# A two-layer graph attention network on one core: one-hot matrices made six at a time, and more edge tiles in two exact parts

## The chip, the core and the metric

The kernel runs on one core of a Trainium2 chip. The core has TensorE (PE, with its weight loads shown apart as PEld), VectorE (DVE), ScalarE (ACT), GpSimd (POOL) and SyncE (SP), which run their own instruction queues in order and wait for one another through semaphores; 16 DMA engines move data between the device memory and the core's SBUF. The metric is device time in microseconds of one execution; lower is better.

## The reference, cut to what matters

The graph has N = 3125 nodes and E = 53125 edges, which are sorted by their target node `dst`. Node features have 768 columns.

```python
h = relu(layernorm(x))
h1 = relu(layer_norm(gat(h, W1, heads=4, 256 columns each))) + h @ Wr1 + br1
out = x + layer_norm(gat(h1, W2, heads=1, 768 columns)) + h1 @ Wr2 + br2

def gat(x, W, ...):
    xl = x @ W
    e = leaky_relu(alpha_src[src] + alpha_dst[dst], 0.2)
    alpha = softmax of e over the edges of one dst        # per head
    return segment_sum(xl[src] * alpha, dst) + bias       # the aggregation
```

The change is in the last line, the aggregation: for every edge the row `xl[src]` is fetched, weighted with the edge's `alpha`, and added to the row of its target node.

## The kernel before, in words

The nodes are cut into NB = 25 blocks of P = 125. Since the edges are sorted, the edges of a block lie in one stretch, and a window of S = 2304 edges, J = 18 tiles of 128, covers it. Edges in the window that belong to other blocks drop out, as their target number relative to the block matches no column.

The function `sums` does the aggregation for both layers, with a loop over the 25 blocks and in it one over the 18 tiles. For one tile `c = b * J + j`:

- L525: POOL issues an indirect DMA that gathers the 128 rows `xl[src]` of the tile from `table` (layer 1: 1024 columns, 4 KB a row; layer 2: 768 columns, 3 KB a row) into a buffer `g`. The row numbers are a column of `idx_s`, which lies in SBUF. Layer 1 has 10 such buffers, layer 2 has 18. Once a block (j = 2) a small indirect DMA `ao` (L531) goes the same way, and once a block SP loads the block's own rows (`own`).
- L536: DVE makes the one-hot matrix `oh` (128 edges x 128 columns) by comparing `iota_f` with the tile's column of `rel_s`, the targets relative to the block. Layer 1 has 8 buffers, layer 2 has 14.
- A tile in two exact parts (`split(j)` true): ACT writes `hi` = `g` x alpha, rounded to the type float32r (L543, four instructions in layer 1, one per head, and one in layer 2); DVE writes the remainder `g` x alpha - `hi` back into `g`, also as float32r (L544, as many instructions). PE multiplies `oh` with the two halves of `hi` and the two halves of `g` (L548), four matmuls, and adds all into the block's PSUM tile `pa`.
- Any other tile: a weight matrix `w` = one-hot x alpha is made, in layer 1 by ACT from `oh`, one per head (L558), in layer 2 by DVE from `iota_f`, `rel_s` and alpha in one instruction (L555), and PE multiplies `w` with `g` in plain float32 (L560). A float32 matmul stands in the trace as two records.

Before the change, layer 1 has one such other tile in each block (j = 8), layer 2 five of 18 (j = 0, 4, 8, 12, 16).

After a block's tiles PE adds the bias (L564). Then `finish` runs for the block while the next block's tiles go on: DVE adds the self-loop (`z`, L512), and layer normalisation follows (L317 to L327). In layer 1, `end1` normalises (L797), transposes on PE (L806), applies relu on ACT (L808), adds the residual on DVE (`h1T`, L810) and multiplies by `W2` on PE (L819); beside it PE works off the residual product `h @ Wr1` for the later blocks (L774), which ends some five blocks before the layer does. In layer 2, `end2` does two instructions of DVE over 768 columns (L908, L909) and stores the result; beside it PE works off the residual product `h1 @ Wr2` of 16 blocks (L853), which DVE adds in L862.

The order on the engines is a scheduler's in layer 1, which places instructions by its own estimates. In layer 2 PE, ACT and DVE keep the order of the program (`lag` is 5: `finish` begins five tiles into the next block), so an instruction that waits holds up all that is queued behind it.

Of the kernel before, what the change touches and what calls it, by code (L numbers as in the profile page):

```python
# [9 lines left out]
F32 = mybir.dt.float32  # L10
F32R = mybir.dt.float32r
# [3 lines left out]
AF = mybir.ActivationFunctionType  # L15
OP = mybir.AluOpType
# [42 lines left out]
def in_order(  # L59
# [16 lines left out]
    nc = tc.nc  # L76
    N, D = x.shape
    E = src.shape[0]
    H, C1 = a_src1.shape
    HC = H * C1  # L80
    C2 = W2.shape[1]
    P = 125
# [10 lines left out]
    table1 = dram.tile([N, HC], F32, name="table1")  # L93
    table2 = dram.tile([N, C2], F32, name="table2")
# [3 lines left out]
    alo1_d = dram.tile([128 * NB * J, H + 1], F32, name="alo1_d")  # L98
    alo2_d = dram.tile([128 * NB * J, 2], F32, name="alo2_d")
# [17 lines left out]
    iota_f = const.tile([128, 128], F32, name="iota_f")  # L117
# [6 lines left out]
    rel_s = const.tile([128, NB * J], F32, name="rel_s")  # L124
# [11 lines left out]
    def load_rows(q, t, src_, b):  # L136


        if b < NB - 1:
            q.dma_start(t, src_[b * P:b * P + 128, :])  # L140
        else:
            q.dma_start(t[:112], src_[b * P:b * P + 112, :])
            q.dma_start(t[112:P], src_[b * P + 112:(b + 1) * P, :])
# [27 lines left out]
    def bias_rows(pool, o, n, name):  # L171
        t = pool.tile([2, n], F32R, name=name)
        nc.sync.dma_start(t.bitcast(F32), parts_d[:, o:o + n])
        return t
# [311 lines left out]
    def sums(heads, cols, table, al, alo_d, bias, split, ahead, his, lag, gp, pp, end, more=iter(())):  # L486

        width = heads * cols  # L490
        f = width // 2
        n = min(cols, f)
        assert split(0) or n == f
        running = []

        def step():
            for g in list(running):
                if next(g, running) is running:
                    running.remove(g)
            next(more, None)  # L500

        def finish(b, own, pa, ao):
            for _ in range(lag):
                yield

            iso = gp.tile([P, 1], F32, name="iso", bufs=2)
            nc.vector.tensor_tensor(iso, ao[:P, heads:], node_f[:P, b:b + 1], OP.not_equal)
            aw = gp.tile([P, heads], F32, name="aw", bufs=2)
            nc.vector.tensor_scalar(aw, ao[:P, :heads], iso, None, op0=OP.max)
            z = gp.tile([P, width], F32, name="z", bufs=2)  # L510
            for o in range(0, width, n):
                nc.vector.scalar_tensor_tensor(z[:, o:o + n], own[:P, o:o + n], aw[:, o // cols:o // cols + 1],  # L512
                                               pa[:, o // f, o % f:o % f + n], op0=OP.mult, op1=OP.add)
            yield from end(b, z)

        with tc.manual_schedule(engines={PE, ACT, DVE}) if lag else nullcontext():
            for b in range(NB):
                own = gp.tile([128, width], F32, name="own", bufs=3 if lag else 2)
                pa = pp.tile([P, 2, 512], F32, name="pa", bufs=2)
                ao = gp.tile([128, heads + 1], F32, name="ao", bufs=3)  # L520
                for j in range(J):
                    c = b * J + j
                    g = gp.tile([128, width], F32R, name="g", bufs=ahead)
                    gf = g.bitcast(F32)
                    nc.gpsimd.indirect_dma_start(  # L525
                        out=gf, out_offset=None, in_=table[:, :],
                        in_offset=bass.IndirectOffsetOnAxis(ap=idx_s[:, c:c + 1], axis=0))
                    if j == 6:
                        load_rows(nc.sync, own, table, b)
                    if j == 2:  # L530
                        nc.gpsimd.indirect_dma_start(  # L531
                            out=ao, out_offset=None, in_=alo_d[:, :],
                            in_offset=bass.IndirectOffsetOnAxis(ap=at_last[:, b:b + 1], axis=0))
                    if split(j) or heads > 1:
                        oh = gp.tile([128, 128], F32R, name="oh", bufs=max(his, 4) + 4)
                        nc.vector.tensor_scalar(oh, iota_f, rel_s[:, c:c + 1], None, op0=OP.is_equal)  # L536
                    if split(j):

                        hi = gp.tile([128, width], F32R, name="hi", bufs=his)
                        for h in range(heads):  # L540
                            cs = slice(h * cols, (h + 1) * cols)
                            a = al[:, j, h, b:b + 1]
                            nc.scalar.activation(hi[:, cs], gf[:, cs], AF.Copy, scale=a)  # L543
                            nc.vector.scalar_tensor_tensor(g[:, cs], gf[:, cs], a, hi[:, cs].bitcast(F32),  # L544
                                                           op0=OP.mult, op1=OP.subtract)
                        for t in (hi, g):
                            for i in range(2):
                                nc.tensor.matmul(pa[:, i, :f], oh[:, :P], t[:, i * f:(i + 1) * f],  # L548
                                                 start=(j == 0 and t is hi), stop=False)
                    else:  # L550
                        w = gp.tile([128, heads, P], F32, name="w", bufs=6 if lag else 4)
                        for h in range(heads):
                            a = al[:, j, h, b:b + 1]
                            if heads == 1:
                                nc.vector.tensor_scalar(w[:, h, :], iota_f[:, :P], rel_s[:, c:c + 1], a,  # L555
                                                        op0=OP.is_equal, op1=OP.mult)
                            else:
                                nc.scalar.activation(w[:, h, :], oh[:, :P].bitcast(F32), AF.Copy, scale=a)  # L558
                        for o in range(0, width, n):
                            nc.tensor.matmul(pa[:, o // f, o % f:o % f + n], w[:, o // cols, :], gf[:, o:o + n],  # L560
                                             start=(j == 0), stop=False)
                    if j == J - 1:
                        for i in range(2):
                            nc.tensor.matmul(pa[:, i, :f], ones_r, bias[:, i * f:(i + 1) * f],  # L564
                                             start=False, stop=True)
                    step()
                running.append(finish(b, own, pa, ao))
            while running:
                step()


    with tc.tile_pool(name="m1", bufs=1) as mp:
        al1 = mp.tile([128, J, H, NB], F32, name="al1")
# [9 lines left out]
        with tc.tile_pool(name="w1", bufs=1) as wp, tc.tile_pool(name="pm1", bufs=1, space=PSUM) as pm1:  # L583
# [131 lines left out]
            with tc.tile_pool(name="pq1", bufs=1, space=PSUM) as pp:  # L715
# [11 lines left out]
                with tc.tile_pool(name="wf", bufs=2) as fp:  # L727
# [3 lines left out]
                    for k in range(NK2):  # L731
                        w2k = fp.tile([128, C2], F32, name="w2k")
                        nc.sync.dma_start(w2k, W2[k * 128:(k + 1) * 128, :])
                        for i in range(2):
                            t = fp.tile([128, C2], F32, name="w2t")
# [14 lines left out]
        with tc.tile_pool(name="w2", bufs=1, reuse_waits="tile") as wp, tc.tile_pool(name="e1", bufs=2, reuse_waits="tile") as ep, \  # L750
                tc.tile_pool(name="g1", bufs=1, reuse_waits="tile") as gp, tc.tile_pool(name="pg1", bufs=1, space=PSUM) as pp:
            w2 = wp.tile([128, NK2, R2], F32, name="w2")
            b1_r = bias_rows(wp, 0, HC, "b1_r")
# [30 lines left out]
            def later():  # L784
                for gi in range(1, NG):
                    yield from residual(gi)
# [5 lines left out]
            def end1(b, z):  # L792
# [32 lines left out]
                        nc.vector.tensor_copy(asad2[:, b, :], pm[:, 384:n])  # L825
                store_rows(nc.sync, table2, b, row)

            sums(H, C1, table1, al1, alo1_d, b1_r, lambda j: j % 18 != 8, 10, 4, 0, gp, pp, end1, later())


    with tc.tile_pool(name="m2", bufs=1, reuse_waits="tile") as mp, \
            tc.tile_pool(name="pr2", bufs=1, space=PSUM, reuse_waits="tile") as pr:
        al2 = mp.tile([128, J, 1, NB], F32, name="al2")
# [63 lines left out]
        more = rest()  # L897

        with tc.tile_pool(name="w3", bufs=1, reuse_waits="tile") as wp, tc.tile_pool(name="e2", bufs=2, reuse_waits="tile") as ep, \
                tc.tile_pool(name="g2", bufs=1, reuse_waits="tile") as gp, tc.tile_pool(name="pg2", bufs=1, space=PSUM, reuse_waits="tile") as pp:  # L900
            b2_r = bias_rows(wp, HC, C2, "b2_r")
            g2_b = wp.tile([P, C2], F32, name="g2_b")
            nc.sync.dma_start(g2_b, bcast(g2, C2))

            def end2(b, z):
                yield from norm_steps(ep, z, C2, 4)
                mu, rstd = norm_steps.found
                nc.vector.scalar_tensor_tensor(z, z, mu, g2_b, op0=OP.subtract, op1=OP.mult)  # L908
                nc.vector.scalar_tensor_tensor(z, z, rstd, xrs[b][:P], op0=OP.mult, op1=OP.add)  # L909
                for _ in range(3):  # L910
                    yield
                store_rows(nc.scalar, out, b, z)

            with tc.issue_after(behind):
                sums(1, C2, table2, al2, alo2_d, b2_r, lambda j: j % 18 not in (0, 4, 8, 12, 16), 18, 10, 5, gp, pp, end2, more)


@with_exitstack
# [469 lines left out]
```

## Time and profile before

| | |
|---|---|
| median of 10 runs | 2423.2 us (2418.51 to 2432.86) |
| the profiled execution | 2423.38 us, span 2421.6 us, mean granted clock 0.955 |
| PE busy | 2233.5 us (92%) |
| DVE busy | 1973.5 us (81%) |
| ACT busy | 1291.9 us (53%) |
| POOL busy | 1188.6 us (49%) |
| DMA | 637.97 MB, mean 263 GB/s |

The stages by time from the span's start: the dense products and softmax of layer 1 up to 512 us, the aggregation of layer 1 from 512 to 1512 us, the softmax of layer 2 up to 1712 us, the aggregation of layer 2 up to the end.

The profile is of one execution. A line of a group names source line, engine, operation, output <- inputs, shapes and count, then the busy time in us and the mean duration of one in ns, then the idle time of the engine just before them with what ended most of it. "issue" is a wait that ended with nothing that the profile shows. Matmuls overlap with their successors, so the duration of one is longer than the time to the next one's start; where the pace of PE matters, the time from start to start is what counts.

### The profile page before, as it was taken

Reading aid. Unit: us, or ns where it says so; the run is one execution under the profiler, and the core shown is the slowest. Engines: PE = TensorE matmul, PEld = TensorE weight load, DVE = VectorE, ACT = ScalarE, POOL = GpSimd, SP = SyncE. Lnnn points to the kernel's source line nnn. Section 1 sums busy time; section 2 is a strip of 40 time slices with the busy share of each in tenths; the row PEclk is TensorE's granted clock in tenths of the full one; section 3 lists DMA queues with packets and bytes.
Section 4 is the critical chain, followed back from the end, with each engine's and each line's share of the span. In section 5 each row is a group of like instructions: output and inputs, shape, how many; then the busy total and the mean of one; then the engine's idle time right before and its main releaser. Section 6 shows DMA issues by size and latency. Waiting matters only on the chain. (4 is left out here: it accounts for less than half of the span.)

```text
span 2421.6 us, 35879 instructions
## 1 busy us (share of the span) xinstructions
PE 2233.5 (92%) x11154; PEld 1457.4 (60%) x11154; DVE 1973.5 (81%) x4429; ACT 1291.9 (53%) x2687; POOL 1188.6 (49%) x1043
## 2 busy tenths in 40 slices
PE   5898999969999999999999999799799999998997
PEld 2565665435666666666666756575466666665665
DVE  6835999678999999989898999587577787777777
ACT  1231333137888888888888987001344444444443
POOL 2100000126756766565555764000577777777774
PEclk8998999989999999999999999799899999998999
DMA  5452552488899898988988986884688898888886
GB/s 182 153 202 91 181 190 62 149 286 295 303 314 305 293 333 292 329 289 309 311 303 284 347 301 223 311 308 143 227 310 307 305 320 303 293 297 302 281 292 212
DMA packets 185691, 637.97 MB, mean 263 GB/s; under 512 B 32170, under 2 KB 49435, under 8 KB 184724
## 3 DMA queue, kind: packets, MB, share of 16 engines
q0 software_dynamic: 109072, 437.23, 53.4%
q1 hardware_dynamic: 72570, 188.75, 22.4%
q10 hardware_dynamic: 3850, 9.60, 1.1%
q8 instruction: 93, 1.52, 0.3%
q14 instruction: 106, 0.87, 0.1%
HBM read 567.40 MB, written 68.08 MB: 262 GB/s over the span
## 5 line engine op out<-in xcount | busy, mean ns | idle before, releaser
L525 POOL DMA_INDIRECT g<-table,idx_s x900 | 1081.0, 1201 | 545.4 <-PE pa L548 296.9
L543 ACT ACTIVATE hi<-g,al 128x256 fp32r<-128x256 f32 (+1 forms) x2025 | 1004.8, 574 | 462.3 <-DMA g<-table,idx_s 183.3
L544 DVE SCALAR_TENSOR_TENSOR g<-g,al,hi 128x256 fp32r<-128x256 f32 (+1 forms) x2025 | 1032.2, 561 | 75.4 <-issue 44.1
L548 PE MATMUL pa<-hi,oh 128*125 128x512 f32 (+1 forms) x1500 | 611.7, 487 | 27.9 <-issue 18.9
L548 PE MATMUL pa<-g,oh 128*125 128x512 f32 (+1 forms) x1500 | 471.1, 389 | 26.0 <-issue 13.1
L548 PEld LDWEIGHTS pa<-hi,oh 128*125 128x125 f32 x1500 | 280.9, 191 | 222.9 <-issue 96.4
L548 PEld LDWEIGHTS pa<-g,oh 128*125 128x125 f32 x1500 | 279.4, 190 | 94.9 <-DVE g L544 28.3
L853 PE MATMUL pr<-wr,h 128*125 128x384 f32 x800 | 303.7, 510 | 16.8 <-issue 13.1
L819 PE MATMUL p<-w,h1T 128*125 128x384 f32 (+1 forms) x800 | 298.0, 492 | 1.8 <-DVE h1T L810 1.5
L645 PE MATMUL pm<-w,h 128*125 128x512 f32 x600 | 284.7, 625 | 0.0
L774 PE MATMUL pr<-h0k,wr 128*128 128x500 f32 (+1 forms) x576 | 257.8, 536 | 17.2 <-DMA h0k<-h0T_d 17.0
L536 DVE TENSOR_SCALAR oh<-iota_f,rel_s 128x128 fp32r<-128x128 f32 x775 | 207.2, 280 | 72.6 <-PE pa L548 71.6
L560 PE MATMUL pa<-g,w 128*125 128x384 f32 (+1 forms) x700 | 243.0, 475 | 13.4 <-ACT w L558 6.9
L853 PEld LDWEIGHTS pr<-wr,h 128*125 128x125 f32 x800 | 152.1, 195 | 105.4 <-issue 36.4
L819 PEld LDWEIGHTS p<-w,h1T 128*125 128x125 f32 x800 | 147.9, 188 | 81.2 <-issue 9.8
L645 PEld LDWEIGHTS pm<-w,h 128*125 128x125 f32 x600 | 114.1, 198 | 126.9 <-issue 126.2
L146 POOL DMA_DIRECT2D table<-row x25 | 16.0, 639 | 349.2 <-ACT row L648 322.2
L560 PEld LDWEIGHTS pa<-g,w 128*125 128x125 f32 x700 | 131.1, 193 | 85.2 <-issue 21.3
L774 PEld LDWEIGHTS pr<-h0k,wr 128*128 128x128 f32 x576 | 105.0, 191 | 60.2 <-DMA h0k<-h0T_d 18.0
L512 DVE SCALAR_TENSOR_TENSOR z<-own,aw,pa 125x256 f32<-125x256 f32 (+1 forms) x150 | 69.9, 521 | 75.9 <-PE pa L548 26.8
L392 PEld LDWEIGHTS <-ohs 125*128 125x128 bf16 x2700 | 101.8, 98 | 47.9 <-DVE ohs L380 32.2
L392 PE MATMUL pq<-tabs,ohs 125*128 125x100 bf16 (+1 forms) x2700 | 105.4, 192 | 22.0 <-DVE ohs L380 19.8
(198 smaller groups left out, 1648.6 us busy)
## 6 DMA issues: line engine op xcount, KB each, us to landing
bd<-dst_d SPq DMA_DIRECT2D x50, 576.0 KB
bs<-slo_d SPq DMA_DIRECT2D x50, 576.0 KB
g<-table,idx_s POOLq DMA_INDIRECT x900
r1T_d<-rt SPq DMA_DIRECT2D x100, 125.0 KB
r1t<-r1T_d SPq DMA_DIRECT2D x25, 500.0 KB
h1T_d<-h1T SPq DMA_DIRECT2D x25, 500.0 KB
h<-h1T_d SPq DMA_DIRECT2D x25, 500.0 KB
own<-table SPq DMA_DIRECT2D x24, 512.0 KB
```

Of the source, the lines that this page charges most:

```text
L392: nc.tensor.matmul(q[:, j], ohs[:P, (j0 + j) * 128:(j0 + j + 1) * 128], tabs[:, i], start=(i == 0), stop=(i == 2))
L512: nc.vector.scalar_tensor_tensor(z[:, o:o + n], own[:P, o:o + n], aw[:, o // cols:o // cols + 1], pa[:, o // f, o % f:o % f + n], op0=OP.m ...
L525: nc.gpsimd.indirect_dma_start(out=gf, out_offset=None, in_=table[:, :], in_offset=bass.IndirectOffsetOnAxis(ap=idx_s[:, c:c + 1], axis=0))
L536: nc.vector.tensor_scalar(oh, iota_f, rel_s[:, c:c + 1], None, op0=OP.is_equal)
L543: nc.scalar.activation(hi[:, cs], gf[:, cs], AF.Copy, scale=a)
L544: nc.vector.scalar_tensor_tensor(g[:, cs], gf[:, cs], a, hi[:, cs].bitcast(F32), op0=OP.mult, op1=OP.subtract)
L548: nc.tensor.matmul(pa[:, i, :f], oh[:, :P], t[:, i * f:(i + 1) * f], start=(j == 0 and t is hi), stop=False)
L560: nc.tensor.matmul(pa[:, o // f, o % f:o % f + n], w[:, o // cols, :], gf[:, o:o + n], start=(j == 0), stop=False)
L645: nc.tensor.matmul(pm[:P], h0[gi][:, k, o:o + P], w1[:, k, i * 512:(i + 1) * 512], start=(k == 0), stop=(k == NK1 - 1))
L774: nc.tensor.matmul(pm[:, :nb * P], wr1[:, k, m * 128:(m + 1) * 128], loaded[gi, k][:, :nb * P], start=(k == 0), stop=(k == NK1 - 1))
L819: nc.tensor.matmul(pm[:, :n], hT[:, k, :], w2[:, k, o:o + n], start=(k == 0), stop=(k == NK2 - 1))
L853: nc.tensor.matmul(pm[:, :384], h1[:, k, :], wr2[:, k, i * 384:(i + 1) * 384], start=(k == 0), stop=False)
```

## The change

The one-hot matrices of six tiles are made by one comparison, a `tensor_tensor` over 6 x 125 columns, with `iota_f` repeated six times and six columns of `rel_s` each repeated 125 times. There are 3 buffers for six tiles each, in both layers, in place of 8 and 14 for one. Each one-hot matrix has 125 columns in place of 128. The comparison is made for every tile, also for those of layer 2 that do not use it. In layer 1 all 18 tiles are now in two parts; in layer 2 all but three (j = 2, 8, 14). `w` has 4 buffers in place of 6 in layer 2.

```diff
-                    if split(j) or heads > 1:
-                        oh = gp.tile([128, 128], F32R, name="oh", bufs=max(his, 4) + 4)
-                        nc.vector.tensor_scalar(oh, iota_f, rel_s[:, c:c + 1], None, op0=OP.is_equal)
+                    if j % 6 == 0:
+
+                        ohs = gp.tile([128, 6, P], F32R, name="oh", bufs=3)
+                        nc.vector.tensor_tensor(ohs, iota_f[:, None, :P].to_broadcast([128, 6, P]),
+                                                rel_s[:, c:c + 6, None].to_broadcast([128, 6, P]), OP.is_equal)
+                    oh = ohs[:, j % 6, :]
...
-                                nc.tensor.matmul(pa[:, i, :f], oh[:, :P], t[:, i * f:(i + 1) * f],
+                                nc.tensor.matmul(pa[:, i, :f], oh, t[:, i * f:(i + 1) * f],
...
-                        w = gp.tile([128, heads, P], F32, name="w", bufs=6 if lag else 4)
+                        w = gp.tile([128, heads, P], F32, name="w", bufs=4)
...
-                                nc.scalar.activation(w[:, h, :], oh[:, :P].bitcast(F32), AF.Copy, scale=a)
+                                nc.scalar.activation(w[:, h, :], oh.bitcast(F32), AF.Copy, scale=a)
...
-            sums(H, C1, table1, al1, alo1_d, b1_r, lambda j: j % 18 != 8, 10, 4, 0, gp, pp, end1, later())
+            sums(H, C1, table1, al1, alo1_d, b1_r, lambda j: True, 10, 4, 0, gp, pp, end1, later())
...
-                sums(1, C2, table2, al2, alo2_d, b2_r, lambda j: j % 18 not in (0, 4, 8, 12, 16), 18, 10, 5, gp, pp, end2, more)
+                sums(1, C2, table2, al2, alo2_d, b2_r, lambda j: j % 18 not in (2, 8, 14), 18, 10, 5, gp, pp, end2, more)
```

## The prediction

> **What bounds the kernel now.** I first cut the span into its stages with the table of windows: the start of layer 1's aggregation (512 to 568 us), its steady part (568 to 1331), its tail after the residual products have run out (1331 to 1512), the softmax of layer 2 (1512 to 1712), layer 2's aggregation (1712 to the end). Columns are the busy us of PE, PEld, DVE, ACT and POOL, then granted clock, DMA share and GB/s.
>
> ```profile
> 568.00:1331.00 763.00, 755.97 (x2697) 485.38 (x2696) 693.32 (x1914) 651.39 (x1619) 476.94 (x370) 1.00 0.90 308
> 1331.00:1512.00 181.00, 172.76 (x690) 117.82 (x690) 172.76 (x480) 160.75 (x410) 112.67 (x82) 0.98 0.84 293
> 1712.00:2422.00 710.00, 634.90 (x2395) 442.88 (x2394) 533.47 (x1057) 303.38 (x349) 514.51 (x471) 0.93 0.86 292
> ```
>
> In the steady part of layer 1, PE is busy 99% at full clock. That alone is weak, since matmuls overlap, so I read who waits for whom in that window:
>
> ```profile
> POOL g L525 <- PE pa L548: 209.0, 204, 2.2
> ACT hi L543 <- PE pa L548: 71.3, 69, 2.8
> DVE oh L536 <- PE pa L548: 51.6, 67, 2.2
> PE pa L560 <- ACT w L558: 4.8, 8, 1.3
> ```
>
> Three engines wait for PE; PE itself waits 4.8 us for the `w` of the one tile per block that goes the fp32 way. PE is the bound there. DVE, at 91%, is next.
>
> Layer 2 is another matter. The groups of that window show 447 gathers, and the waits of POOL there show how little it is held up:
>
> ```profile
> L525 POOL DMA_INDIRECT g<-table,idx_s x447 | 486.5, 1088 | 168.1 <-issue 95.7 <-PE pa L548 33.3 <-remote 15.8
> POOL g L525 <- issue: 95.7, 314, 0.3
> POOL g L525 <- PE pa L548: 33.3, 56, 2.6
> ```
>
> POOL issues one gather of 128 rows after another, about 1.09 us each with 0.305 us between: 471 x (1.092 + 0.305) = 658 of 710 us. It waits for PE 33 + 5 us. So gather issue sets layer 2's pace, with the PE and DVE loop just behind it. Last, the timeline shows what makes an issue long (start us, us):
>
> ```profile
> 1952.27 0.95 POOL L525 DMA_INDIRECT g<-table,idx_s  x1 [0.30 <-issue]
> 1957.29 1.02 DVE L909 SCALAR_TENSOR_TENSOR z<-z,bn_rs,xr 125x768 f32<-125x768 f32 x1
> 1957.39 1.74 POOL L525 DMA_INDIRECT g<-table,idx_s  x1 [0.30 <-DVE z L908]
> ```
>
> An undisturbed issue takes 0.95 us. The second one began while a DVE instruction on two SBUF tensors ran until 1958.31, and ended 0.82 us after that. From start and end times, 110 of the 456 issues between 1730 and 2400 us end 0.82 us after an L544 ends and are longer by 54 us together; 30 do so after an L536, by 2.2 us.
>
> **The change, part by part.**
>
> PE, layer 1: 25 tiles (j = 8) leave the fp32 path. In the chain, `PE pa L560 x8` takes 1.73 us up to the next start. Four split matmuls of 512 columns: the timeline has two of them at 860.22 and the next two at 860.68, so 0.23 each, 0.93 us a tile. Saved 0.80 us a tile, on the path for the 19 blocks of the steady part and the first block: 20 x 0.80 = 16.0 us. The wait of 4.8 us for `w` goes; I count 3, since `hi` comes in its place.
>
> DVE, layer 1, per block: 18 `oh` at 0.258 (89.4 us over 347) go, -4.6. Three comparisons of 128x750 come. No row has this shape; the same form at 128x450 (L382) takes 0.617 us and a product of 128x1024 (L308) 1.217, which bound it; by the line through both, 0.93, so +2.6 with the overlap of 0.08 of neighbouring instructions. Four L544 at 0.413 (535.7 over 1297) come, +1.7. Sum -0.4 us a block. The window holds 19.1 blocks of 39.9 us (counted from one block's first L512 to the next's), so DVE goes from 693.3 / 19.1 = 36.3 to 35.9 while the block goes to some 39.0. ACT gets four `hi` at 0.42 for four `w` at 0.32, +0.4 on 34.1.
>
> Does DVE's lead over PE survive? In the order of the built program the comparison for tiles 12 to 17 stands behind tile 2 and waits for the previous block's last matmul. Queued behind it is `z` (L512), which waits for the same matmuls, so no wait is added; but `z` and tiles 3 to 7 come 0.93 - 0.28 = 0.65 us later. From start and end times, `g` of tile 6 is ready 1.17 us before PE takes it (the smallest lead in a block), tile 10 3.05. Afterwards 0.5 at tile 6; at tile 10, 3.05 - 1.65 (g of tile 8) - 0.8 (faster PE) - 0.65 + 0.84 (three `oh` gone) = 0.6. Thin but positive. If it fails, each us short is a us of PE idle; I take 2 us for it in all, between 0 and 16.
>
> The tail is DVE's (172.8 of 181): 5 blocks x 0.4 = 2 us. Layer 1: -16 - 3 - 2 + 2 = -19 us.
>
> PE, layer 2: 50 tiles change over. Four fp32 matmul records of 384 columns last 1.45 us at 0.486 each, so they start 0.32 apart: 1.29 us a tile; in the chain `PE pa L548 x12` takes 2.10, 0.175 each: 0.70 a tile. Saved 50 x 0.59 = 29 us of PE. But POOL, not PE, has the path; this pays at most the 40 us that POOL waits for PE, and at most 29. Between 0 and 29 I take 13, for POOL was held in only 64 of its 447 issues.
>
> DVE, layer 2, per block: -13 x 0.277 - 2 x 0.342 + 3 x 0.93 + 2 x 1.012 = +0.5 us on 21.5 of 27.3. Hidden in DVE's idle quarter. ACT +2 x 0.934 on some 12, hidden too. A comparison needs its buffer's old tiles, at nearest 13 tiles back, done by PE; `hi` with 10 buffers already keeps DVE within 12.
>
> POOL, layer 2: what DVE now does holds it up more. Per L544 the delay is 54 / 325 = 0.165 us; 50 more make +8. The 75 comparisons have two SBUF inputs and 0.93 us, nearest to L544: 75 x 0.165 x (0.93/1.01)^2 = +11. The 325 `oh` go: -2. Sum +17. Ends: +6, if the comparisons with their repeated inputs hold nothing; +37, if every issue meets DVE at a random moment (half an instruction of 1.01 us out of every 1.46 us between issues, so 0.35 an L544 and 0.29 a comparison, less 2).
>
> On this the Trainium skill, "SBUF — State Buffer", section "Who interferes with whom", says that a DVE instruction with two SBUF inputs contends with a GpSimd instruction that reads SBUF, and a two-port one with any; it speaks against this change. The rows above agree for L544 and L909; by it the comparisons hold POOL like L544, +17, and without it the sum of layer 2 would lose its 11. The same section infers that a tensor_tensor does not hold up descriptor writing, which the 1.74 us row does not bear out for its kind of instruction.
>
> Layer 2: +17 - 13 = +4 us. SP's queue keeps its order; on POOL a few gathers of `ao` change places with neighbours in `g`, which I cost at nothing while no `ao` is needed for five tiles; uncovered it would be one issue, 1.4 us.
>
> Sum: -19 + 4 = -15 against the profiled execution's 2423.38 us (span 2421.6 and 1.8 around it), which is within 0.2 us of the median of the ten runs, 2423.2: **2408 us**. What this kernel can tell from no change is about 0.2%, 4.8 us.
>
> **Rivals.**
>
> Forecast (0.50): layer 1 gains most of PE's 16 to 21 us, layer 2 stays within 10 us of where it is: 2398 to 2418.
>
> PE relief reaches layer 2 as well (0.17): the PE and DVE loop, not POOL, is what the chain of waits mostly walks through there (PE pa L548 26.9% of the window, POOL L525 1.8%). With +8 from POOL and -24 from PE: -35, 2388. Against it: POOL's gaps are 0.305 in most issues.
>
> Slower (0.20): DVE takes the gather issue. Place: the 471 issues of layer 2; price: the mean excess over 0.95 us, 0.15 now; the forecast takes it to 0.18. At the random bound it is 0.23, +37, and with POOL as sole bound nothing of PE's relief is paid: -19 + 37 = +18, 2441. It decides from 19 us net, 0.04 us an issue; over 24 us, 0.05 an issue, the kernel is slower. For it: POOL has no slack in layer 2. Against: issues now meet L544 only about half as often as at random.
>
> No difference (0.13): layer 1's lead of 0.5 us isn't there, DVE takes over the pace and gains only its 0.4 us a block there and in the tail, some -9; layer 2 at +4 to +9: 2418 to 2423. That the change doesn't do what it says is out: the built order has 18 pairs of `hi` and `g` matmuls in each block of layer 1 and 15 in layer 2.
>
> **How the numbers follow.** Likeliest case 2408; its own range 2398 to 2418. Down to 2390 takes in most of the second case, up to 2430 the undecided one and the milder half of the slower one. Faster by over 0.2% is the first two: 0.66, as the little of the first that lies above 2418 is made up by the last; same 0.13; slower 0.21.
>
> **What would show it.** Right: layer 1 blocks of some 39 us, no L560 records of 256 columns, comparisons at 0.93 us; POOL's mean issue in layer 2 at 1.12 us or so. Wrong: `pa L548 <- DVE g L544` growing past 10 us between 568 and 1331; POOL's mean issue over 1.15; or POOL's waits for PE in layer 2 gone with the mean unchanged, which is the second case.

## The result, and the profile after

The change made the kernel slower. The changed kernel takes 2506.6 us (median of 11 runs, 2497.1 to 2521.5), the kernel before 2425.5 on the same chip (40 runs): ratio 1.0344, 95% interval 1.0329 to 1.0360. The forecast was 2408, its range ended at 2430. The profiled execution has a span of 2496.7 us, 75.1 more than before.

Where the 75 us lie. A block's `z` is the first of its `z` instructions (L512); first and last `z` are those of the first and the last block of a layer:

| stretch | before | after | difference |
|---|---|---|---|
| start to layer 1's first `z` | 568.4 | 560.9 | -7.5 |
| first to last `z` of layer 1 | 942.3 | 999.6 | +57.3 |
| last `z` of layer 1 to first of layer 2 | 245.0 | 240.6 | -4.4 |
| first `z` of layer 2 to the end | 665.9 | 695.6 | +29.7 |

So both layers lost, layer 1 most. Of layer 1's 57 us, 23 lie in the first 19 blocks (41.3 us a block for 40.1) and 34 in the last five (42.8 for 36.0). The three stages in the table of windows, columns as before (PE, PEld, DVE, ACT, POOL, clock, DMA share, GB/s):

```profile
568.00:1331.00 763.00, 738.92 (x2552) 455.01 (x2551) 679.09 (x1653) 635.71 (x1577) 624.81 (x350) 1.00 0.83 294
1331.00:1512.00 181.00, 154.67 (x599) 105.84 (x597) 151.41 (x365) 139.92 (x353) 137.81 (x79) 0.92 0.77 272
1712.00:2422.00 710.00, 631.19 (x2389) 434.19 (x2388) 558.34 (x757) 329.65 (x375) 527.57 (x437) 0.94 0.83 273
```

In layer 1's steady part, PE, DVE and ACT are all less busy than before, and DMA moves 294 GB/s in place of 308. One engine is busier: POOL, 625 us in place of 477, with fewer instructions (350 for 370). The waits of that window:

```profile
POOL g L525 <- issue: 61.3, 195, 0.9
ACT hi L546 <- DMA g<-table,idx_s: 56.4, 36, 5.2
DVE g L547 <- ACT hi L546: 55.6, 33, 4.9
POOL g L525 <- PE pa L551: 48.7, 100, 4.8
PEld pa L551 <- DVE g L547: 38.3, 72, 4.7
```

Before, three engines waited for PE. Now the waits run the other way: ACT for the gathered rows, up to 5.2 us at a time, DVE for ACT, PE for DVE. POOL's own wait for PE has shrunk from 209 to 49 us. The gathers come late because issuing one takes longer. The group of the gathers in the same window, before and then after (busy us, mean ns | idle before them):

```profile
L525 POOL DMA_INDIRECT g<-table,idx_s x348 | 455.9, 1310 | 262.9 <-PE pa L548 209.0 <-issue 40.6 <-PE pa L560 12.5
```

```profile
L525 POOL DMA_INDIRECT g<-table,idx_s x329 | 601.8, 1829 | 121.0 <-issue 61.3 <-PE pa L551 48.7 <-PE pr L777 4.3
```

The mean issue went from 1.31 to 1.83 us. Of layer 1's 475 indirect DMAs, 50 now take over 4 us, against 8 before; the longest takes 12.37 us (10.79 in the window). The timeline of POOL shows how they sit (start us, us):

```profile
864.07 4.75 POOL L525 DMA_INDIRECT g<-table,idx_s  x1 [0.59 <-PE pa L551]
869.12 3.85 POOL L525 DMA_INDIRECT g<-table,idx_s  x1 [0.30 <-PE pa L551]
873.27 9.20 POOL L525 DMA_INDIRECT g<-table,idx_s  x1 [0.31 <-issue]
882.78 0.94 POOL L525 DMA_INDIRECT g<-table,idx_s  x1 [0.30 <-PE pr L777]
```

The same stretch on DVE:

```profile
869.90 1.66 DVE L547 SCALAR_TENSOR_TENSOR g<-g,al,hi 128x256 fp32r<-128x256 f32 x4
871.49 0.67 DVE L813 TENSOR_TENSOR h1T<-h1T,r1t 128x500 f32<-128x500 f32 x1
872.08 9.58 DVE L547 SCALAR_TENSOR_TENSOR g<-g,al,hi 128x256 fp32r<-128x256 f32 x24
...
886.35 1.68 DVE L547 SCALAR_TENSOR_TENSOR g<-g,al,hi 128x256 fp32r<-128x256 f32 x4 [4.69 <-ACT hi L546]
```

DVE runs 24 remainders back to back, six tiles, from 872.08 to 881.66. The issue that began in that time ends at 882.47, 0.81 us after the last of them. It held up the supply of six tiles; from 881.66 DVE then stands idle for 4.69 us and waits for data. Before the change an `oh` stood, as a rule, between the remainders of two tiles. Now one comparison serves six tiles, and nothing need stand there. From start and end times of blocks 1 to 19 of layer 1, the mean chain of remainders had 4.5 before (largest 15) and 6.3 after (largest 28); the average remainder stood in a chain of 7.7 before and 12.2 after.

In layer 2 the answering lines are the group and POOL's waits:

```profile
L525 POOL DMA_INDIRECT g<-table,idx_s x413 | 499.8, 1210 | 125.9 <-issue 65.2 <-PE pa L551 25.3 <-DMA g<-table,idx_s 10.7
```

```profile
POOL g L525 <- issue: 65.2, 214, 0.3
POOL g L525 <- PE pa L551: 25.3, 83, 0.3
```

An issue there takes 1.21 us in place of 1.09, and no gap is longer than the fixed 0.305: the longest was 3.6 before. Gather issue now sets layer 2's pace alone: 19 x (1.207 + 0.305) = 28.7 us a block (1.207 with `ao`), measured 28.5, before 27.3.

### The profile page after: what moved, and what is told of

Its sections match the earlier page's. It is cut to its first block, busy times and chain, and to the rows that moved or that the text cites. A ratio compares the mean times of both kernels' runs of the same rounds, so it can differ in the third digit from the quotient of the medians.

```text
span 2496.7 us, 34907 instructions
## 1 busy us (share of the span) xinstructions
PE 2240.5 (90%) x11054; PEld 1438.5 (58%) x11054; DVE 2024.2 (81%) x3904; ACT 1345.7 (54%) x2737; POOL 1459.0 (58%) x1043
## 4 chain that ended last, share of the span: by engine, by line
PE 39%; DVE 26%; DMA 16%; issue 11%; ACT 4%; POOL 3%; SPq 1%; ACTq 0%; another core or an unknown queue 0%; DVEq 0%; POOLq 0%
DMA g<-table,idx_s 14%; PE pa L551 11%; DVE g L547 9%; PE p L822 5%; PE pm L648 5%; PE pr L856 5%; PE pr L777 4%; ACT hi L546 3%; POOL g L525 3%; PE pq L392 2%; DVE oh L537 2%; PE pa L563 2%; DVE scr L394 2%; PE pm L747 2%; DVE al L397 2%
## 5 line engine op out<-in xcount | busy, mean ns | idle before, releaser
L525 POOL DMA_INDIRECT g<-table,idx_s x900 | 1351.7, 1502 | 363.8 <-issue 163.2
L546 ACT ACTIVATE hi<-g,al 128x256 fp32r<-128x256 f32 (+1 forms) x2175 | 1095.7, 579 | 566.7 <-DMA g<-table,idx_s 347.2
L547 DVE SCALAR_TENSOR_TENSOR g<-g,al,hi 128x256 fp32r<-128x256 f32 (+1 forms) x2175 | 1108.3, 569 | 256.2 <-ACT hi L546 192.4
L551 PE MATMUL pa<-hi,oh 128*125 128x512 f32 (+1 forms) x1650 | 656.1, 478 | 66.9 <-DVE oh L537 28.0
L551 PE MATMUL pa<-g,oh 128*125 128x512 f32 (+1 forms) x1650 | 562.0, 409 | 79.0 <-DVE g L547 56.3
L551 PEld LDWEIGHTS pa<-hi,oh 128*125 128x125 f32 x1650 | 309.2, 194 | 280.9 <-issue 122.2
L537 DVE TENSOR_TENSOR oh<-iota_f,rel_s 128x750 fp32r<-128x750 f32 x150 | 138.9, 927 | 5.0 <-PE pa L551 5.0
L563 PE MATMUL pa<-g,w 128*125 128x384 f32 x300 | 123.4, 538 | 0.0
L651 ACT ACTIVATE row<-pm 125x512 f32<-125x512 f32 x50 | 29.8, 595 | 151.5 <-PE pm L648 138.7
L531 POOL DMA_INDIRECT ao<-alo_d,at_last x50 | 56.7, 1134 | 86.3 <-DMA alo_d<-own 58.4
```

The lines of the kernel that those rows point to most:

```text
L525: nc.gpsimd.indirect_dma_start(out=gf, out_offset=None, in_=table[:, :], in_offset=bass.IndirectOffsetOnAxis(ap=idx_s[:, c:c + 1], axis=0))
L531: nc.gpsimd.indirect_dma_start(out=ao, out_offset=None, in_=alo_d[:, :], in_offset=bass.IndirectOffsetOnAxis(ap=at_last[:, b:b + 1], axis=0))
L537: nc.vector.tensor_tensor(ohs, iota_f[:, None, :P].to_broadcast([128, 6, P]), rel_s[:, c:c + 6, None].to_broadcast([128, 6, P]), OP.is_equal)
L551: nc.tensor.matmul(pa[:, i, :f], oh, t[:, i * f:(i + 1) * f], start=(j == 0 and t is hi), stop=False)
```

## The experiments

The kernel before takes about 2425 us on the chips of the first result, of e9 and e10, and of the last sweep, and 2382 to 2385 us on those of the other runs. So ratios are compared, each to the kernel before on the run's own chip, and stage times within one chip. Theory A is that DVE's chains of two-input instructions hold up gather issue; the main rival is that PE's saving was never there, or was lost to DVE's load and order.

**Both kernels again, on the second chip.** `a0_after` is the changed kernel, `b0_before` one execution of the kernel before.

> The changed kernel, unchanged, on the same chip. All theories: ratio about 1.034; if theory A is right, layer 2's block is 19 x (mean issue + 0.305) us to within 0.5 us on any chip.

Ratio 1.0462 (1.0435 to 1.0489), larger than on the first chip. First to last `z` of layer 1: 941.3 before, 981.7 after, +40. First `z` of layer 2 to the end, less than on the first chip only for the kernel before: 632 and 700 us, +68. The windows of 1760 to 2330 us show it. The kernel before moves 318 GB/s there and the changed one 290:

```profile
1760.00:2330.00 570.00, 542.35 (x2114) 374.06 (x2112) 466.60 (x923) 268.27 (x306) 444.39 (x413) 0.99 0.92 318
```

```profile
1760.00:2330.00 570.00, 505.03 (x1900) 351.32 (x1899) 448.95 (x631) 279.57 (x315) 456.22 (x374) 0.93 0.88 290
```

On the first chip the same two windows show 300 and 291. There the kernel before had 21 gaps over 0.4 us between its issues in the layer, 32 us above 0.305 in sum; here it has none. The changed kernel has none on either. On the first chip these waits went as the issue grew longer, so the layer lost less than the issue gained. A layer 2 block takes 28.7 us here and 25.9 before, by 19 x (mean issue + 0.305) 29.0 and 26.2, as theory A expected. Stage times rest on one execution each: e5 and e8 below have the layer 2 of the kernel before on the same kind of chip and take 643 and 637 us there, for the 632 here. In layer 1 the first 19 blocks lost 6 us here and the last five 35.

**One half of the change at a time.** `e1_parts_only` has the new sets of tiles in two parts and keeps `oh` tile by tile; `e2_six_only` has the comparison of six tiles and the old sets.

```diff
 e1, against the kernel before:
-            ... lambda j: j % 18 != 8, 10, 4, 0, ...
+            ... lambda j: True, 10, 4, 0, ...
-                ... lambda j: j % 18 not in (0, 4, 8, 12, 16), 18, 10, 5, ...
+                ... lambda j: j % 18 not in (2, 8, 14), 18, 10, 5, ...
 e2, against the changed kernel: the same two lines, taken back
```

> The changed set of tiles in two exact parts (all 18 of layer 1, 15 of 18 of layer 2), with the one-hot matrices made one by one as before. Theory A (POOL is shut out by unbroken chains of DVE instructions with two SBUF inputs, and the per-tile comparisons used to break the chains): the breaks are back, so layer 1 gains PE's saving and the mean gather issue of layer 1 stays near 1.3 us; 2400 to 2425 us. Rival B (the 75 more tiles in two parts overload DVE and ACT): as slow as the changed kernel, about 2500 us. Rival C (the comparison of six tiles comes as a lump of 0.93 us and with three shared buffers, so DVE loses its lead over PE): the lump is gone, 2400 to 2420 us.

> The comparison of six tiles alone, with the old set of tiles in two parts (17 of 18 and 13 of 18). A: the chains are as unbroken as in the changed kernel but for one tile a block; the mean issue of layer 1 is 1.6 us or more, 2465 to 2500 us. B: no more parts than before and less DVE work, 2415 to 2425 us. C: 2480 to 2505 us, with the mean issue of layer 1 near 1.3 us.

The parts alone: 0.9999 (0.9980 to 1.0018). The comparison alone: 1.0253 (1.0210 to 1.0295). In e2 47 issues of layer 1 take over 4 us, in e1 one. With e1, blocks 1 to 19 of layer 1 take 38.86 us, the forecast's "some 39". So PE's saving in layer 1 was real, and there the comparison of six tiles is what cost; in layer 2 the parts cost as well, which is why e1 as a whole gains nothing. The two are not additive: 0 and 2.5% make 4.6 together (on another chip of the same kind).

**One comparison per tile, of the new kind.** Is it the kind of instruction (two SBUF inputs) or the breaks that are missing? `e3_tt_each` and `e7_tt_each_8` differ in `bufs` alone, 18 and 8.

```diff
-                    if j % 6 == 0:
-                        ohs = gp.tile([128, 6, P], F32R, name="oh", bufs=3)
-                        nc.vector.tensor_tensor(ohs, ...[128, 6, P]..., OP.is_equal)
-                    oh = ohs[:, j % 6, :]
+                    ohs = gp.tile([128, 1, P], F32R, name="oh", bufs=18)
+                    nc.vector.tensor_tensor(ohs, ...[128, 1, P]..., OP.is_equal)
+                    oh = ohs[:, 0, :]
```

> The changed kernel with one tensor_tensor comparison per tile (128x125, about 0.28 us) in place of one per six tiles, 18 buffers of one tile. A: a comparison with two SBUF inputs is a break as well, for POOL got in at the end of every such comparison in the changed kernel: 2405 to 2435 us, mean issue of layer 1 at most 1.4 us. If only another kind of instruction (one SBUF input) makes a break: about 2500 us. B: about 2500 us. C: 2400 to 2420 us.

> The changed kernel with one comparison of 128x125 (tensor_tensor, two SBUF inputs) per tile in place of one of 128x750 for six tiles, as in e3_tt_each, but with 8 buffers in place of 18, so that the comparisons can't run far ahead and must stand between the remainders of neighbouring tiles. Theory A1 (any other instruction between the four remainders of a tile lets the gather issue in, whatever its inputs): mean issue in layer 1 falls to 1.3 to 1.45 us with fewer than 15 over 4 us, chains of remainders average about 4, layer 1 blocks 38.8 to 39.1 us, ratio to the kernel before 1.005 to 1.015 (what is left is layer 2). Theory A2 (only an instruction with a single SBUF input lets it in, so comparisons of this kind prolong the chain): mean issue stays at 1.6 to 1.8 us, over 30 above 4 us although the chains of remainders are short, blocks 40 us or more, ratio 1.02 to 1.035. Rival B (DVE's load and order, not the shut-out): DVE does 18 comparisons of some 0.24 us a block, 1.5 us a block more than with three long ones; blocks over 40 us with a mean issue below 1.4 us.

e3 missed theory A's range: 1.0225 (1.0185 to 1.0265), mean issue in layer 1 1.65 us. With 18 buffers the scheduler let the comparisons run ahead in bunches, and chains of up to 23 remainders stayed. With 8 buffers the chains are as short as with `oh` (mean 3.9, largest 15, the same as in e1), and all of theory A1's numbers hold: mean issue 1.42 us, 4 over 4 us, blocks of 38.91 us, ratio 1.0119 (1.0086 to 1.0153). From start and end times, some 260 of the 475 issues end 0.82 us after such a comparison. So a two-input comparison between two tiles lets POOL in as well, but not always. The longest issue of all runs is in e7, in the last blocks of layer 1:

```profile
1460.37 14.05 POOL L525 DMA_INDIRECT g<-table,idx_s  x1 [0.30 <-issue]
```

Six comparisons and two of `h1T`, all with two SBUF inputs, ran to their end in that time, between groups of four remainders. In the runs whose breaks are the one-input `oh` or the copy of e4 (the kernel before, e1, e4, e5, e8), no issue was held past such a break.

**A small break.** `e4_small_break` is the changed kernel with a copy of one column behind the second remainder of each tile of layer 1, an instruction that nothing uses.

```diff
+                            if heads > 1 and h == 1:
+                                nop = gp.tile([128, 2], F32, name="nop", bufs=4)
+                                nc.vector.tensor_copy(nop[:, :1], hi[:, cs][:, :1].bitcast(F32))
```

> The changed kernel with one more DVE instruction in each tile of layer 1: a copy of one column of hi into a tile that nobody reads, behind the second of the four remainders, so that no chain is longer than four. A: POOL gets in at each, the mean issue of layer 1 falls from 1.77 to below 1.3 us, and layer 1 wins back its 50 us in spite of the added work; layer 2 stays as slow as it is: 2440 to 2460 us. B and C: DVE only gets more work, some 0.1 us a tile: 2506 to 2550 us.

Ratio 1.0138 (1.0099 to 1.0176) against 1.0462 without the copies, measured on another chip of the same kind. DVE does 354 instructions more in the steady part, 0.145 us each, and everything else there is faster (groups and waits of 568 to 1331 us):

```profile
L525 POOL DMA_INDIRECT g<-table,idx_s x356 | 412.0, 1157 | 321.6 <-PE pa L554 306.0 <-issue 12.2 <-PE pr L780 1.9
```

```profile
568.00:1331.00 763.00, 763.00 (x2732) 488.51 (x2732) 739.50 (x2114) 681.31 (x1682) 433.12 (x378) 1.00 0.91 317
```

No issue takes over 4 us, POOL is back to waiting for PE, and PE is busy without a gap, with blocks of 39.0 us. The last five blocks are back at 36.8 us, for 42.8. DVE's lead over PE therefore held, and the rival of load and order falls. A timeline of DVE there:

```profile
870.05 0.93 DVE L537 TENSOR_TENSOR oh<-iota_f,rel_s 128x750 fp32r<-128x750 f32 x1
870.89 0.87 DVE L547 SCALAR_TENSOR_TENSOR g<-g,al,hi 128x256 fp32r<-128x256 f32 x2
871.69 0.14 DVE L551 COPY nop<-hi 128x1 f32<-128x1 f32 x1
871.75 1.66 DVE L547 SCALAR_TENSOR_TENSOR g<-g,al,hi 128x256 fp32r<-128x256 f32 x4
873.33 0.14 DVE L551 COPY nop<-hi 128x1 f32<-128x1 f32 x1
```

**One SBUF input.** `e6_one_input` is the changed kernel with the remainder replaced by `g` x alpha alone, over one column less; the subtraction is left out.

```diff
-                            nc.vector.scalar_tensor_tensor(g[:, cs], gf[:, cs], a, hi[:, cs].bitcast(F32), ...)
+                            cd = slice(h * cols, (h + 1) * cols - 1)
+                            nc.vector.tensor_scalar(g[:, cd], gf[:, cd], a, None, op0=OP.mult)
```

> The changed kernel with the DVE remainder (g x alpha - hi, two SBUF inputs) replaced in both layers by g x alpha over one column less, an instruction of about the same length with one SBUF input; the subtraction of hi is left out, so the sums count a tile in two parts about twice. DVE's load, ACT, PE and all buffers stay. A: POOL is no longer shut out; mean issue near 1.0 us in both layers, layer 1 back to blocks of 38.5 to 39.5 us, layer 2 to 25 to 26.5 us a block; ratio 0.96 to 0.985. B and C: the load and the lumps are the same, so the time is that of the changed kernel, ratio about 1.03.

Ratio 0.9789 (0.9764 to 0.9814), mean issue 1.06 us in layer 1 and 1.07 in layer 2. The test takes away more than one thing, for the one-input form is also shorter: 0.374 us in place of 0.475 in layer 1, 0.637 for 1.014 in layer 2; in the last five blocks of layer 1 this saves 18 us against e4, so not all of the ratio is the issue. What separates the two is a chain of it, in which POOL isn't held (DVE, then POOL):

```profile
858.98 6.03 DVE L548 TENSOR_SCALAR g<-g,al 128x255 fp32r<-128x255 f32 x17
```

```profile
860.48 0.94 POOL L525 DMA_INDIRECT g<-table,idx_s  x1 [0.61 <-PE pa L551]
863.53 0.94 POOL L525 DMA_INDIRECT g<-table,idx_s  x1 [2.11 <-PE pa L551]
```

Over layer 1, issues that began beside such an instruction (it ran 0.08 us after the issue's start) with eight or more of the chain, this one included, still to run took 1.08 us here (64 issues, 48 of them undisturbed) and 4.39 in the changed kernel (82 issues, 14 undisturbed).

**Layer 1 alone.** `e5_layer1_parts` has all 18 tiles of layer 1 in two parts and is otherwise the kernel before; `e8_break_layer1` has layer 1 as e4 and layer 2 as before.

> The part of the change that the runs so far speak for: one-hot matrices one by one, all 18 tiles of layer 1 in two parts, layer 2 as in the kernel before. A: layer 1 keeps PE's saving (blocks of 38.9 us), layer 2's mean issue goes back to 1.09 us; 15 to 20 us faster than before, ratio about 0.993. B: 25 more tiles in two parts, slower by some 10 us. C: as A in layer 1.

> Layer 1 with the comparison of six tiles, all 18 tiles in two parts and the one-column copy behind the second remainder of every tile, as in e4_small_break; layer 2 exactly as in the kernel before (one-hot matrices tile by tile, 13 of 18 tiles in two parts). If layer 1 and layer 2 add up: layer 1 as e4_small_break (blocks 38.9 to 39.1 us, tail 37.2, mean issue about 1.14 us, first to last z some 923 us against 941 before), layer 2 as before (mean issue 1.07 to 1.09 us), so about 18 to 22 us less than the kernel before, ratio 0.990 to 0.994, the same as e5_layer1_parts within 0.3%: then the comparison of six tiles by itself pays nothing even where POOL gets in. If the comparison of six tiles does pay once POOL isn't shut out: 0.985 or less. If what e4_small_break gained came from something other than layer 1's issue: ratio near 1.0.

0.9902 (0.9882 to 0.9922) and 0.9915 (0.9885 to 0.9944). Both beat both kernels, by layer 1 alone: first to last `z` 921.5 and 923.0 us, against 941.3. That they agree shows that the comparison of six tiles gains nothing in layer 1 even where it does no harm: the steady part is then PE's. In the tail, which is DVE's, the copies take back what the comparison saves DVE (18 x 0.145 = 2.6 us a block), so a gain there isn't excluded.

**How many tiles of layer 2 in two parts.** From e5, with 11 and 9 of 18 in place of 13.

```diff
-... lambda j: j % 18 not in (0, 4, 8, 12, 16), 18, ...
+... lambda j: j % 18 not in (0, 2, 5, 8, 11, 14, 16), 18, ...    (11; with 9: j % 2 == 1)
```

> e5_layer1_parts (one-hot matrices tile by tile, layer 1 with all 18 tiles in two parts) with 11 of layer 2's 18 tiles in two parts in place of 13: the step of the change in layer 2, taken backwards. Going from 13 to 15 raised layer 2's issue time over 0.945 us by 20 us (70.6 in e5_layer1_parts, 90.9 in e1_parts_only), 0.4 us a tile. Theory A (gather issue sets layer 2's pace, PE has room): excess falls by 20 to about 50 us, mean issue 1.05, layer 2 block down by 0.8 us to some 25.5, ratio to the kernel before 0.980 to 0.985 (e5_layer1_parts 0.990). Rival (PE is close enough behind that its 0.59 us for each tile taken back, 29 us, is paid): mean issue falls the same, but the waits of gathers for PE grow and the block is 26.3 to 27.5 us, ratio 0.990 to 1.003.

> As e9_layer2_11 with 9 of 18 tiles of layer 2 in two parts (every second one). Theory A: another 20 us of issue time less, mean issue 1.02, block about 25, ratio 0.970 to 0.978. Rival (PE sets the pace by now): block 27 us or more, gathers of layer 2 wait for PE for more than 100 us, ratio 0.998 to 1.015.

0.9940 (0.9922 to 0.9959) and 0.9894 (0.9868 to 0.9920), with mean issues of 1.050 and 1.025 us as expected, but blocks of 27.2 and 27.0. So theory A missed its blocks and ratios in both runs: issue alone would make 25.8 and 25.3. The rival's ranges hold e9 and the block of e10, not e10's ratio, and gathers waited for PE for some 67 us there, not over 100. That chip was a slower one, on which the kernel before has waits too, so a sweep on one chip was added:

> Sweep on one chip, 1 of 4: one-hot matrices tile by tile, layer 1 with 18 of 18 tiles in two parts, layer 2 with 15 of 18 (the same kernel as e1_parts_only). Theory I (layer 2 is set by gather issue, block = 19 x (mean issue + 0.305)): mean issue 1.136, block 27.1 to 27.4 on any chip. Theory P (where the chip is slow enough that gathers wait for buffers, PE's 0.59 us a tile is paid): block not longer than with 13 of 18. On a chip of the faster kind: ratio 0.998 to 1.002; on one of the slower kind (before at 2425 us) 0.985 to 0.992, since before's waits of 35 us go.

> Sweep, 2 of 4: layer 2 with 13 of 18 (the same kernel as e5_layer1_parts), layer 2 therefore as in the kernel before. Theory I: mean issue 1.09, block 26.3 on a chip of the faster kind, ratio 0.990 (layer 1 alone). On a chip of the slower kind waits of some 35 us stay in layer 2 and block is 27.3, ratio 0.990 too, as layer 2 is the same in both.

> Sweep, 3 of 4: layer 2 with 11 of 18. Mean issue 1.05. If waits for buffers (some 50 us, as in e9_layer2_11's profile) come from the chip: on a faster one they go, block 25.7, ratio 0.98 to 0.985. If they come from PE's longer work: block 27 on either kind of chip, ratio 0.994 or above, slower than with 13.

> Sweep, 4 of 4: layer 2 with 9 of 18. Mean issue 1.025. If the waits come from the chip: block 25.3 on a faster one, ratio 0.975 to 0.98. If from PE's longer work: block 27 or more, ratio 0.989 or above on either kind.

The chip was again one on which the kernel before takes 2425 us. Ratios with 15, 13, 11 and 9: 0.9921, 0.9905, 0.9897, 0.9897, with intervals of about 0.003 to each side: no difference. Mean issue falls from 1.125 to 1.034 us, and blocks stay at 27.5, 27.5, 27.3 and 27.1. Two windows, 15 first and then 9:

```profile
1760.00:2330.00 570.00, 510.98 (x1990) 367.19 (x1988) 472.13 (x905) 279.92 (x323) 436.17 (x385) 0.93 0.89 297
```

```profile
1760.00:2330.00 570.00, 553.93 (x1997) 362.91 (x1996) 365.85 (x783) 173.69 (x205) 403.64 (x391) 0.99 0.89 301
```

PE's busy time differs by 43 us, DVE's by 106. By 19 x (mean issue + 0.305) the blocks would be 27.2, 26.5, 25.7 and 25.5. With 15 tiles issue nearly fills the block; with fewer, the time won goes into longer gaps between the issues (21 us above 0.305 with 15 tiles, 53 with 9). So on this chip something else holds layer 2 near 27 us a block once issue is shorter than that. The waits name mostly buffers that PE has yet to free, but in these four kernels PE's work grows as issue shrinks, by about the same amount, so they don't separate PE from the rate at which rows arrive (297 to 301 GB/s in all four). What it is wasn't tested, nor were 11 and 9 tiles on a faster chip.

## Why the prediction was wrong

The step that failed is one that isn't there: layer 1's sum has terms for PE, `w`, the tail and DVE's lead, and none for POOL. Gather issue was weighed in layer 2 alone.

| step | forecast, us | measured |
|---|---|---|
| PE in layer 1, with `w` | -19 | -25 in the first 19 blocks (e5, 736.9 for 761.9) |
| a comparison of 128x750 | 0.93 each | 0.927 |
| DVE's lead over PE | +2 | no loss (e4: PE 763.00 of 763.00); the prediction's sum for tile 10 is 0.8, not 0.6 |
| tail of layer 1, last five blocks | -2 | +5 (e5, 184.6 for 179.4); +34 and +35 in the changed kernel |
| gather issue in layer 1, tail included | no term | -20 (e5, 921.5 for 941.3) became +57 on the first chip, +40 on the second |
| gather issue in layer 2 | +17 | +55 and +69 |
| relief of waits in layer 2 | -13 | -32 on the first chip, none on the second, which had no such waits |

**Layer 1.** POOL waited 209 us for PE there, and I took that for room enough. But every gather waits 0.305 us in any case. All idle time before the gathers was 262.9 / 348 = 0.76 us each, so the slack was some 0.45. The mean issue rose by 0.52, which alone uses it up: 18 x (1.829 + 0.305) + 1.4 for `ao` = 39.8 us a block, against 38.9 that PE needs. Issues of up to 10.8 us, with ten buffers ahead of PE, are the likely rest: 41.3. The tail, to which the prediction gave -2, lost more than the steady part; three of the four longest issues, 12.37 and twice 10.05 us, lie there. That e4 brings both parts back shows that the cause is the same. The profile had the warning. By the method of the prediction's last fence, applied to layer 1, 143 of the 271 disturbed issues of the kernel before end some 0.89 us after a remainder which an `oh` follows. The `oh` that the change removes were the places at which POOL got in. I counted them as DVE time only, 4.6 us a block to be saved.

**Layer 2.** The mechanism was named, the term was a third of its size or less. The price of a meeting hardly changed: counted by the DVE instruction that ran 0.08 us after an issue's start, an issue that began beside a remainder was 0.39 us longer before and 0.40 after. What was wrong is the number of meetings. Remainders rose from 325 to 375 and the comparisons came to 75, but issues that began beside a remainder rose from 147 to 237. Before, 124 began beside an `oh` or a one-instruction `w`, which cost them 0.04 and 0.02 us. These harmless places went with the change, and the "-2" for the 325 `oh` was the wrong sign. The comparisons themselves came out as forecast: 27 meetings of 0.49 us, 13 us for my 11. Some 9 us more came from the first instruction of `end2` (L908, L911 after): 15 issues began 0.2 us into it and were held 0.67 us each; before, one of the 19 beside it was held. Nor was the random bound of +37 an upper end: it counted the new instructions alone, and by its own price the 325 old remainders could cost another 325 x (0.35 - 0.165) = 60 us.

By e1 and e2 the parts raise the excess of layer 2 over 0.945 us an issue by some 24 us and the comparison by some 44 (90.9 and 111.3 against a mean of 67.4 in five runs with layer 2 as before).

**The rivals.** The slower one, at 0.20, had the right mechanism, the wrong place (layer 2 alone) and a price of +37 that was too small; its 2441 is 66 us short. "No difference", by way of DVE's lead, is refuted by e4 and e8. That PE's relief makes layer 2 faster did not come: the layer lost 30 us. How much of the waits that went on the first chip is PE's relief isn't shown; in the sweep PE's work and the issue change against each other.

**The rule on two SBUF inputs.** Of what the prediction took from the Trainium skill, "SBUF — State Buffer", section "Who interferes with whom", the rule that a DVE instruction with two SBUF inputs contends with a GpSimd instruction that reads SBUF was the better guide, and I used it for one layer. The trace agrees in detail. In layer 2 of the changed kernel, 215 issues began 0.1 us or more into a remainder, a comparison or an instruction of `end2`, with 0.2 us or more of it left: none was undisturbed, and 212 end 0.8 us after it. The undisturbed ones (4 of 27 beside a comparison, 59 of 237 beside a remainder) began at its very start or end. Beside `z` (L512), whose second tensor lies in PSUM, all 21 were undisturbed. The page speaks of a lock for one instruction; the 9.20 us row is 21 of them long. Its inference that a tensor_tensor leaves descriptor writing alone doesn't help for these gathers: their issue is held beside one. As the issue also reads its row numbers from SBUF, the runs don't tell which of the two is held.

**What stays open.** A chain doesn't always hold POOL. Of the 82 issues of layer 1 that began with eight or more remainders still to come, 14 were undisturbed (all of these began at the very start or end of a remainder), 19 were let in at the end of the instruction that was running, and 26 only at the end of the chain, the rest elsewhere. What decides between these was not found, nor why a two-input comparison in the chain mostly, but not always, ends the hold. The runs show that a chain without a break can hold an issue to its end, and that the one-input `oh` and the copy of e4 ended the hold each time.

## What to carry to other kernels

Before you merge small instructions of VectorE into a large one, look at what else got in between them: here a 0.26 us instruction per tile was what let GpSimd issue its gathers in time. A queue that only waits still has a budget, so work out its slack per item, without the gap that it has in any case (here some 0.45 us), and check it against what each neighbour's new order can take from it. Where two changes come together, time them apart: of the one half here, a part (layer 1's tiles, e5) is worth 1%, and the other half by itself costs 2.5% (e2).

## What the runs showed of the hardware

- Short VectorE instructions with two SBUF inputs, back to back at 0.40 us, can hold a GpSimd gather issue of 0.95 us for the whole chain, up to 12.4 us in the changed kernel; a 0.145 us copy in the chain of every tile brought the mean issue of layer 1 from 1.77 to 1.14 us (e4 against a0).
- The same chain with one SBUF input doesn't do so (1.08 us against 4.39), though in layer 2 the one-input instruction of 767 columns still delays an issue that begins beside it: 147 issues, 1.11 us on average.
- In layer 2 of the changed kernel an issue that began inside an instruction with two SBUF inputs ended 0.8 us after it (212 of 215); beside one whose second input lies in PSUM none was held (21 of 21).
- Two-input comparisons between the remainders of neighbouring tiles mostly end the hold (mean issue 1.42 us in e7), but one issue of 14.05 us lasted through six of them.
- Chips differ in layer 2: the kernel before moves 300 GB/s between 1760 and 2330 us on one and 318 on another, and with it the same change costs 3.4% or 4.6%.
